# A guess dealt out in single operations over ScalarE, in the second step of a sparse-attention graph layer

## The chip, the core and the metric

One core of a Trainium2 chip runs the kernel. The metric is device time in microseconds (us). Engines are named as in the profile: PE (TensorE, matrix products and transposes), DVE (VectorE), ACT (ScalarE), POOL (GpSimd), SP (SyncE, which issues DMAs).

## What is computed

The input is x (3327 nodes, 256 features) and a sparse matrix adj. After a layer norm and a ReLU, two steps run; each has an attention over all nodes that keeps, for every row, the largest probabilities until their sum passes 0.9:

```
q = X @ W1.T @ W2.T ;  k = X @ W3.T
probs = softmax(q @ k.T)                 # one row per node
keep the largest probs of a row while the sum of those before is < 0.9
A = kept probs / their sum
for n in range(2):
    A  = top_p_attention(Xa)
    Xf = R @ Xf          # R: adj + identity, rows scaled to sum 1
    Xa = A @ Xa
    Z  = Z + Xf @ U1[n].T + Xa @ U2[n].T
out = x + layernorm(X + Z) * g + b
```

## The kernel before

The 3327 nodes are padded to 26 tiles of 128 rows; "a row" below is one such tile, and e is its 128 x 3328 array of exponentials. Every row goes through the same stages, which are Python generators, and the stages of neighbouring rows are interleaved.

`weights` makes e: PE multiplies query and keys (L591), and ACT takes the Exp of four quarters (L601 for three, L609 and L611 for the fourth with its last column apart); the sums go to the columns of `za`.

`measured_twice` (second step) finds a first threshold. It begins with `guessed`: on ACT, small operations on 128 x 1 columns of a tile g, each reading the one before it (L621 to L626), and two more, L675 and L676. POOL then forms three columns (L677 to L679). Now come three passes of ACT over the whole e, each line L634 with a sum per row: one Relu and one Sign at the guessed threshold, then, after two small ACT operations (L688, L689) that read DVE's L686 and L687, a second Sign at a better threshold. DVE (L698, L700, and L706 to L717), POOL (L690 to L693) and ACT (L702 to L704) compute from the three sums a last value, and ACT's L719 makes of it the column that the next stage compares with.

`settle` finds the exact threshold on DVE: a pass over e (L734), 20 searches for the eight largest of a piece (L739), rounds of search and replacement (L746, L750), and a last pass over e (L776) that sets to zero what is not kept.

`Sums` transposes e on PE in pieces of four tiles (pt, L822), copies them on ACT (eT, L824) and multiplies with the nodes (pa, L836). `spread` multiplies the gathered neighbours (pr, L942), and `finish` (L991 on) makes the output row. In the opening of the second step the last rows of the first are closed (L959 to L962), and `laws` computes on PE and DVE constants for all rows (L548 to L554).

The order of each engine's queue is the order of the text, and that is written by hand: each row has seven parts, and for each part a string of letters says which generator is advanced by one yield. In the second step w is `weights` two rows ahead, m `measured_twice` of the next row, n what is left of it from the row before, d `settle`, f `finish`, s `spread`, l `laws`, g the fetching of neighbours; `PLAN[1]` holds the strings of the rows that repeat, `OPEN` those of the first rows, `LAST` those of the last.

Of the kernel before, what the change touches and what calls it, by code (L numbers as in the profile page):

```python
# [9 lines left out]
F32 = mybir.dt.float32  # L10
# [3 lines left out]
AF = mybir.ActivationFunctionType  # L14
# [4 lines left out]
P = 128  # L19
# [327 lines left out]
def guess_graph_layer(ctx, tc, x, adj, w1t, w2t, w3t, u1t, u2t, ln_g, ln_b, out, flag):  # L347
# [9 lines left out]
    small = ctx.enter_context(tc.tile_pool(name="small", bufs=4))  # L357
# [5 lines left out]
    V, G, S, PE = nc.vector, nc.gpsimd, nc.scalar, nc.tensor  # L363

    rows_of = lambda t: min(P, N - t * P)
    valid = lambda t: 0 <= t < NT
# [206 lines left out]
    def weights(step, t, live, known=True):  # L573

        r = dict(Z=rec[:, step, 3, t : t + 1])
        qT = asked(t)
        yield
        r["ms"] = law_of(t) if known and step else early.get(t)
        lawful = law_once(step, t) if known and not step else none
        r["e"] = e = es[(2, 3, 0, 1, 4, 5)[t % 6] if step else t % 4]  # L580
        r["za"] = za = small.tile([P, CUT + 1], F32, tag="za", name="za")
        live[step, t] = r
        w = HALF * P
        wd = w // CUT
        pls = {}

        def product(n):
            pls[n] = pl = ps_l.tile([P, 2, 512], F32, tag="pl", name="pl")
            for a in range(2):
                p = slice(a * DA, (a + 1) * DA)  # L590
                PE.matmul(pl[:, a, :wd], qT[p, :],  # L591
                          keys_of(step, a).rearrange("p a b -> p (a b)")[:, n * wd : (n + 1) * wd],
                          start=True, stop=True)

        for n in range(CUT):
            c = n * wd
            if n not in pls:
                product(n)
            pl = pls.pop(n)
            if n < CUT - 1:  # L600
                S.activation(e.rearrange("p (a n) -> p a n", a=2)[:, :, c : c + wd], pl[:, :, :wd],  # L601
                             AF.Exp, accum_out=za[:, n : n + 1])
                if known and not step and n < 2:
                    r["ms"] = returned(lawful) if n else next(lawful)
                if known and step and n == CUT - 2:
                    product(n + 1)
                yield
            else:
                S.activation(e.rearrange("p (a n) -> p a n", a=2)[:, :, c : w - 1], pl[:, :, : wd - 1],  # L609
                             AF.Exp, accum_out=za[:, n : n + 1])  # L610
                S.activation(e[:, w - 1 : w], pl[:, 0, wd - 1 : wd], AF.Exp, accum_out=za[:, n + 1 :])  # L611

    def guessed(r, g, step):

        r["col"] = col = lambda k: g[:, k : k + 1]
        ms = r["ms"]  # L620
        S.activation(r["za"], r["za"], AF.Copy, accum_out=r["Z"])  # L621
        S.activation(col(0), r["Z"], AF.Ln)
        S.activation(col(2), col(0), AF.Relu, scale=-0.25, bias=ms(7))
        S.activation(col(2), col(2), AF.Exp, scale=-1.0, bias=con((6, 9)[step]))
        S.activation(col(3), col(2), AF.Square, bias=con((3, 8)[step]))
        S.activation(col(9), col(3), AF.Exp, scale=ms(3), bias=ms(8))  # L626
        return col

    def con(k):
        return one[:, k : k + 1]  # L630
# [5 lines left out]
    def measured_once(r):  # L636
        e, ms = r["e"], r["ms"]


        col = guessed(r, small.tile([P, 17], F32, tag="g", name="g"), 0)  # L640
        S.activation(col(4), col(2), AF.Square, bias=con(4))
        S.activation(col(11), col(4), AF.Identity, scale=ms(5), bias=ms(6))
        S.activation(col(1), col(0), AF.Exp, scale=-1.0, bias=con(5))
# [25 lines left out]
    def measured_twice(r):  # L669
        e, ms = r["e"], r["ms"]  # L670

        col = guessed(r, small.tile([P, 18], F32, tag="g", name="g"), 1)
        S.activation(col(1), col(0), AF.Exp, scale=-1.0, bias=con(5))  # L675
        S.activation(col(11), col(2), AF.Square, bias=con(4))  # L676
        G.tensor_scalar(col(11), col(11), ms(5), ms(6), ALU.mult, ALU.add)  # L677
        G.tensor_scalar(col(5), col(1), OFFSET[1], None, ALU.mult)  # L678
        G.tensor_scalar(col(7), col(3), ms(3), ms(8), ALU.mult, ALU.add)  # L679
# [6 lines left out]
        V.tensor_scalar(col(3), oa[:, 1:2], float(NP), col(9), ALU.add, ALU.mult)  # L686
        V.tensor_scalar(col(4), col(3), 0.5, oa[:, 0:1], ALU.mult, ALU.subtract)  # L687
        S.activation(col(6), col(4), AF.Ln, scale=col(1), bias=con(2))  # L688
        S.activation(col(13), col(6), AF.Exp, scale=col(11), bias=col(7))  # L689
        G.tensor_scalar(col(14), col(13), col(9), 0.25, ALU.add, ALU.mult)  # L690
        G.tensor_scalar(col(10), col(13), col(5), 1.0, ALU.mult, ALU.add)
# [8 lines left out]
        V.tensor_scalar(d1, col(15), col(4), 0.0, ALU.add, ALU.max)  # L700
        V.tensor_scalar(col(0), oa[:, 2:3], NP - 61.0, BIG, ALU.is_gt, ALU.mult)
        S.activation(col(2), d1, AF.Abs, scale=col(1), bias=con(1))  # L702
        S.activation(col(2), col(2), AF.Ln, scale=0.2, bias=col(10))
        S.activation(col(3), d1, AF.Ln, scale=col(1), bias=con(2))  # L704
        yield
        V.tensor_scalar(col(12), col(4), d1, 1.0e-30, ALU.subtract, ALU.add)  # L706
# [258 lines left out]
    def first_end(t):  # L965
        if t >= NT - ENDS:
            last = t == NT - 1
            aT = adjp.tile([P, AD, P], F32, tag="at", name="aT", bufs=2)[:, :ND, :] if last else None
            aT = transposed(live.pop(("r", t)), xT=aT, copy=V.tensor_copy if last else S.copy)
            ends.append((t, aT))  # L970
            stores()
            yield
            yield from prep(aT, t, V.tensor_copy if last else S.copy)
            return
        aT = transposed(live.pop(("r", t)))
        stores()
        yield
        pz = ps_r.tile([P, 2 * D], F32, tag="pr", name="pz")
        for c in range(ND):
            PE.matmul(pz, aT[:, c, :], u2[:, c].rearrange("p n d -> p (n d)"), start=c == 0, stop=c == ND - 1)  # L980
        S.copy(xw[:, t, :], pz[:, D:])
        sv = row.tile([P, D], F32, tag="sv", name="sv", bufs=2)
        S.copy(sv, pz[:, :D])
        G.tensor_tensor(sv, sv, x0[:, t, :], ALU.add)
        yield
        kept[t] = sv
        yield from prep(aT, t)
# [36 lines left out]
    none = iter(())  # L1024
# [3 lines left out]
    def run(work, n=99):  # L1028
        for _ in range(n):
            next(work, None)  # L1030
# [137 lines left out]
    def refetch(t):  # L1168
# [7 lines left out]


    ROUNDED = "dsdfdfddfd"
    CLOSED = "mdmwdmdmdmdmdmd"
    PLAN = (("gmdsssa", "gmcdsssa", "edawwpg", "gmsdga", "gmspdea", "ohgdawwqg", "gehmgq"),  # L1180
            ("llcmss", "lnms", "lwwnfd", "lcmdsssgggg", "fdmwqd", "llm" + ROUNDED, "l" + CLOSED + "g"))

    LAST = {NT - 1: ("cfss", "cn", "nd", "sss", "f" + "d" * 5 + "sdf" + "d" * 11, "ff", ""),
            NT: ("c", "", "", "ff", "ff", "ffv", "f"),
# [4 lines left out]
             NT + 1: ("", "weweee", "", "", "", "", ""),  # L1189
             2: ("gmdsssa", "gmcdsssga", "gedawwpg", "gmsdga", "gmspdea", "ohgdawwqg", "gehmgq")}  # L1190
    OPEN = {-1: ("mxx", "mxl", "mxlggg", "mgxl", "mwxl", "m" * 7 + "l", "lmlggg"),
            0: ("cmssggg", "lnms", "wwnfd", "cmdsss", "fdmgwqd", "m" + ROUNDED, CLOSED),
            1: ("cmss", "nms", "wwnfd", "cmdsssgggg", "fdmwqd", "mg" + ROUNDED, CLOSED + "g")}
    OPEN[2] = OPEN[3] = OPEN[1]
    spacing = itertools.chain(spaced((0, 1)), *(spaced((t,)) for t in range(2, NT)))
    fetching = itertools.chain(*(refetch(t) for t in range(NT)))
# [22 lines left out]
    for step in range(2):  # L1219
        sums = Sums(step, live, xw if step else x0, AHEAD[step])  # L1220

        for i in range(-1, NT + 2):
# [4 lines left out]
            if step == 1 and i == -1:  # L1227
# [6 lines left out]
                m=measured(step, live[step, i + 1]) if valid(i + 1) else none,  # L1234
                s=spread(step, i - 2 + 2 * step) if valid(i - 2 + 2 * step) and (step or i < NT) else none,
                w=later.pop((step, i + 2), none),
                e=first_end(i - 2) if step == 0 and valid(i - 2) else none,
                a=itertools.islice(lister, 6) if step == 0 else none,
                p=packed(i + 1) if step == 0 and i >= 0 and valid(i + 1) else none,
# [112 lines left out]
```

## Time and profile before

| | |
|---|---|
| median of 3 runs | 1324.24 us (1319.92 to 1325.54) |
| the profiled execution | 1318.72 us, span 1316.6 us |
| second step, rows that repeat | from 795.5 to 1250.2 us of the span |
| busy share of the span | PE 95%, DVE 87%, ACT 81%, POOL 69% |

Times in the profile are us from the span's start. A row of a timeline reads: start, duration, engine, line, operation, what is written <- what is read, shape, count, and in brackets the idle time before it with what ended it. A small operation's duration can reach into the next one's start, so that the distance of two starts says what an operation takes of its engine; the chain of waits shows it cut in this way. A matmul of 32-bit values is counted twice.

### The profile page before, as it was taken

To read this page: it belongs to the slowest core of one execution; us is meant where nothing else is said; L and a number is where in the kernel's file an instruction comes from. 1 tells how busy PE (TensorE), PEld (TensorE's weight loads), DVE (VectorE), ACT (ScalarE), POOL (GpSimd) and SP (SyncE) were. 2 spreads that over 40 slices of the span, in tenths; PEclk is the share of its full clock that TensorE was granted. 3 is DMA by queue.
4 is the path that set the end of the run, shared out by engine and by line. 5 is a ranking of instruction groups with operands and counts; after the bars stand their busy time and mean duration, and the time that the engine had idled before them with its cause. 6 is when DMAs were issued, how large, how long until landed. Compare 5 with 4: busy or idle time off the path is not lost.

```text
span 1316.6 us, 22157 instructions
## 1 busy us (share of the span) xinstructions
PE 1254.5 (95%) x6396; PEld 958.4 (73%) x6396; DVE 1141.8 (87%) x3674; ACT 1070.2 (81%) x2304; POOL 914.7 (69%) x1226
## 2 busy tenths in 40 slices
PE   5989899999999999999999869999999999999995
PEld 4635677777877778777777547877777777777874
DVE  6867799999999999999994499899998999989993
ACT  5375788798888888888873779999999999999951
POOL 6114788888878888888785466776776767677632
PEclk9999999999999999999999969999999999999998
DMA  7734555455555555554533321322313222131200
GB/s 249 264 118 137 156 143 148 139 158 149 145 149 149 145 161 136 144 161 143 151 87 104 94 70 51 105 68 84 96 55 101 62 89 93 59 100 56 91 21 23
DMA packets 100723, 153.13 MB, mean 116 GB/s; under 512 B 16849, under 2 KB 67152, under 8 KB 100592
## 3 DMA queue, kind: packets, MB, share of 16 engines
q1 hardware_dynamic: 83056, 108.72, 26.0%
q0 software_dynamic: 16640, 42.69, 12.9%
q8 instruction: 53, 0.87, 0.3%
q14 instruction: 78, 0.64, 0.2%
q10 hardware_dynamic: 896, 0.21, 0.1%
HBM read 120.88 MB, written 27.28 MB: 113 GB/s over the span
## 4 chain that ended last, share of the span: by engine, by line
PE 54%; ACT 33%; DVE 8%; issue 2%; POOL 1%; DMA 0%; DVEq 0%; ACTq 0%; POOLq 0%; SPq 0%
PE pa L836 23%; ACT ja L634 15%; PE pl L591 8%; PE pt L822 6%; PE pr L942 5%; ACT eT L824 4%; PE pz L980 3%; ACT e L601 3%; PE pz L1053 3%; ACT x L601 1%; DVE cand L739 1%; PE pk L1097 1%; DVE w L734 1%; PE pk L481 1%; ACT e L609 1%
## 5 line engine op out<-in xcount | busy, mean ns | idle before, releaser
L634 ACT ACTIVATE ja<-e,g 128x3328 uint8<-128x3328 f32 x106 | 325.7, 3073 | 0.2
L836 PE MATMUL pa<-xw,eT 128*128 128x256 f32 x1352 | 321.3, 382 | 3.1 <-DVE s L991 3.1
L836 PE MATMUL pa<-x,eT 128*128 128x256 f32 x1352 | 321.7, 379 | 0.1
L836 PEld LDWEIGHTS pa<-xw,eT 128*128 128x128 f32 x1352 | 250.8, 190 | 48.8 <-DVE cand L739 13.2
L836 PEld LDWEIGHTS pa<-x,eT 128*128 128x128 f32 x1352 | 242.8, 190 | 25.9 <-ACT xa L845 0.4
L739 DVE MAX8 cand<-w 128x8 f32<-128x168 f32 (+1 forms) x1040 | 253.3, 317 | 0.0
L824 ACT COPY eT<-pt 128x512 f32<-128x512 f32 (+1 forms) x364 | 198.5, 553 | 44.7 <-PE pt L822 43.0
L913 POOL DMA_INDIRECT ac<-in_adj,index x130 | 187.8, 1444 | 58.1 <-issue 17.6
L934 POOL DMA_INDIRECT xg<-bx,index x130 | 184.1, 1416 | 48.1 <-issue 16.9
L822 PE MATMUL pt<-ident,e 128*128 128x128 f32 x1144 | 176.2, 276 | 6.3 <-DVE e L773 2.9
L822 PEld LDWEIGHTS pt<-ident,e 128*128 128x128 f32 x1144 | 138.5, 143 | 59.9 <-issue 33.1
L734 DVE SCALAR_TENSOR_TENSOR w<-e,g 128x3328 f32<-128x3328 f32 x44 | 162.5, 3692 | 1.0
L934 POOL DMA_INDIRECT xg<-vx,index x130 | 128.8, 991 | 34.3 <-issue 25.1
L942 PE MATMUL pr<-xg,ac 128*128 128x257 f32 (+1 forms) x520 | 141.5, 396 | 11.0 <-DVE s L1161 7.0
L776 DVE SCALAR_TENSOR_TENSOR e<-e,rec 128x3328 f32<-128x3328 f32 x40 | 147.2, 3680 | 0.6
L601 ACT ACTIVATE e<-pl 128x832 f32<-128x832 f32 x132 | 113.9, 865 | 28.2 <-PE pl L591 28.2
L942 PEld LDWEIGHTS pr<-xg,ac 128*128 128x128 f32 x520 | 93.5, 194 | 38.8 <-issue 15.4
L591 PE MATMUL pl<-both,qT 64*128 64x416 f32 x416 | 99.6, 543 | 7.7 <-ACT e L601 4.3
L591 PE MATMUL pl<-after,qT 64*128 64x416 f32 x416 | 89.5, 544 | 0.0
L678 POOL TENSOR_SCALAR g<-g 128x1 f32<-128x1 f32 x26 | 83.5, 3213 | 1.8
L866 DVE TENSOR_REDUCE fm<-at 128x4 f32<-128x512 f32 (+1 forms) x133 | 84.3, 634 | 0.0
L677 POOL TENSOR_SCALAR g<-g,law 128x1 f32<-128x1 f32 x23 | 25.1, 1093 | 81.3 <-ACT g L676 81.3
(273 smaller groups left out, 2052.1 us busy)
## 6 DMA issues: line engine op xcount, KB each, us to landing
at<-in_adj SPq DMA_DIRECT2D x114, 256.0 KB
cx<-ac SPq DMA_DIRECT2D x26, 384.0 KB
ac<-cx SPq DMA_DIRECT2D x26, 384.0 KB
wide<-in_adj SPq DMA_DIRECT2D x8, 832.0 KB
e<-in_adj SPq DMA_DIRECT2D x6, 832.0 KB
own<-bx SPq DMA_DIRECT2D x26, 128.5 KB
x<-in_x SPq DMA_DIRECT2D x13, 256.0 KB
qT<-both SPq DMA_DIRECT2D x104, 32.0 KB
```

The costliest lines, as they stand in the source:

```text
L591: PE.matmul(pl[:, a, :wd], qT[p, :], keys_of(step, a).rearrange("p a b -> p (a b)")[:, n * wd : (n + 1) * wd], start=True, stop=True)
L601: S.activation(e.rearrange("p (a n) -> p a n", a=2)[:, :, c : c + wd], pl[:, :, :wd], AF.Exp, accum_out=za[:, n : n + 1])
L634: S.activation(ja, e, f, bias=guess, scale=sign, accum_out=total)
L734: V.scalar_tensor_tensor(w, e, col(16), e, ALU.is_lt, ALU.mult, accum_out=d2)
L739: V.max(cand[:, 8 * s : 8 * s + 8], w[:, s * SEG : min(NP, (s + 1) * SEG)])
L776: V.scalar_tensor_tensor(e, e, at(1), e, ALU.is_ge, ALU.mult, accum_out=ra)
L822: PE.transpose(pt[:, j, :], e[:, (j0 + j) * P : (j0 + j + 1) * P], ident)
L824: S.copy(eT[:, :w, :], pt[:, :w, :])
L836: PE.matmul(self.pa, eT[:, c - 4 * k, :], self.xa[:, j, :], start=c == 0, stop=c == NT - 1)
L913: G.indirect_dma_start(out=ac[:, k, :], out_offset=None, in_=rows, in_offset=bass.IndirectOffsetOnAxis(ap=index[:, t, k : k + 1], axis=0), ...
L934: G.indirect_dma_start(out=xg[:, k, :w], out_offset=None, in_=rows, in_offset=bass.IndirectOffsetOnAxis(ap=index[:, t, k : k + 1], axis=0))
L942: PE.matmul(pr[:, :w], ac[:, k, :], own if k == KT - 1 else xg[:, k, :w], start=k == 0, stop=k == KT - 1)
```

## The change

Only the second step is touched. What `guessed` did there is now a generator of its own, `guessing`, with one operation per yield; `weights` makes it when the fourth Exp is issued. A new letter z advances it, for the row two ahead. The operations are the same eight, with the one that makes column 1 moved into the middle and the last two swapped; their lines are now L619 to L632. In `measured_twice` there are more yields: the first resumption runs what is left of the first six operations, the second the last two and POOL's three; the Ln and the Exp of the old L688 and L689 (now L716 and L718) stand in two resumptions, as do the old L702, L703 and L704 (now L731, L733, L735). The old L719 is L750. In part 4 the strings now resume w twice, with one m between them, so that the fourth Exp comes there and no longer in part 6. The first step computes what it did before.

```diff
@@ weights: at its end
+                if step:
+                    r["chain"] = guessing(r)
+
+    def guessing(r):
+        r["col"] = col = lambda k, g=small.tile([P, 18], F32, tag="g", name="g"): g[:, k : k + 1]
+        ms = r["ms"]
+        S.activation(r["za"], r["za"], AF.Copy, accum_out=r["Z"])
+        yield
+        S.activation(col(0), r["Z"], AF.Ln)
+        yield
+        S.activation(col(2), col(0), AF.Relu, scale=-0.25, bias=ms(7))
+        yield
+        S.activation(col(1), col(0), AF.Exp, scale=-1.0, bias=con(5))
+        yield
+        S.activation(col(2), col(2), AF.Exp, scale=-1.0, bias=con(9))
+        yield
+        S.activation(col(3), col(2), AF.Square, bias=con(8))
+        yield
+        S.activation(col(11), col(2), AF.Square, bias=con(4))
+        S.activation(col(9), col(3), AF.Exp, scale=ms(3), bias=ms(8))
+
+    def guess_of(t):
+        for _ in live[1, t]["chain"]:
+            yield
@@ measured_twice
-        col = guessed(r, small.tile([P, 18], F32, tag="g", name="g"), 1)
-        S.activation(col(1), col(0), AF.Exp, scale=-1.0, bias=con(5))
-        S.activation(col(11), col(2), AF.Square, bias=con(4))
+        chain = r.pop("chain")
+        if "col" not in r:
+            run(chain, 5)
+        next(chain)
+        col = r["col"]
+        yield
+        run(chain)
...
         S.activation(col(6), col(4), AF.Ln, scale=col(1), bias=con(2))
+        yield
         S.activation(col(13), col(6), AF.Exp, scale=col(11), bias=col(7))
...
         S.activation(col(2), d1, AF.Abs, scale=col(1), bias=con(1))
+        yield
         S.activation(col(2), col(2), AF.Ln, scale=0.2, bias=col(10))
+        yield
         S.activation(col(3), d1, AF.Ln, scale=col(1), bias=con(2))
@@ the strings
-    CLOSED = "mdmwdmdmdmdmdmd"
+    CLOSED = "zmdmzmzdmmdmdmdmdmd"
-            ("llcmss", "lnms", "lwwnfd", "lcmdsssgggg", "fdmwqd", "llm" + ROUNDED, "l" + CLOSED + "g"))
+            ("llcmnmss", "lms", "lwwnfd", "lcmdsssgggg", "fdwmwmqd", "llzmz" + ROUNDED, "l" + CLOSED + "g"))
-            0: ("cmssggg", "lnms", "wwnfd", "cmdsss", "fdmgwqd", "m" + ROUNDED, CLOSED),
-            1: ("cmss", "nms", "wwnfd", "cmdsssgggg", "fdmwqd", "mg" + ROUNDED, CLOSED + "g")}
+            0: ("cmmssggg", "lnms", "wwnfd", "cmdsss", "fdwmgwmqd", "zmz" + ROUNDED, CLOSED),
+            1: ("cmnmss", "ms", "wwnfd", "cmdsssgggg", "fdwmwmqd", "zmzg" + ROUNDED, CLOSED + "g")}
@@ where the generators are set
+                z=guess_of(i + 2) if step and i > 0 and valid(i + 2) else none,
```

ACT in a row that repeats, from its second pass to its third; before, the two small operations come first and one Exp (the third) after them:

```order
L634 ACTIVATE ja,oa<-e_100,g 128x3328
L824 COPY eT<-pt 128x512
L688 ACTIVATE g<-g,one 128x1
L689 ACTIVATE g<-g 128x1
L601 ACTIVATE x_95,za<-pl 128x2x416
L824 COPY eT<-pt 128x512
L634 ACTIVATE ja,oa<-e_100,g 128x3328
```

and now:

```order
L658 ACTIVATE ja,oa<-e_100,g 128x3328
L855 COPY eT<-pt 128x512
L601 ACTIVATE x_95,za<-pl 128x2x416
L716 ACTIVATE g<-g,one 128x1
L609 ACTIVATE x_95,za<-pl 128x2x415
L611 ACTIVATE x_95,za<-pl 128x1
L718 ACTIVATE g<-g 128x1
L855 COPY eT<-pt 128x512
L619 ACTIVATE za,rec<-za 128x5
L658 ACTIVATE ja,oa<-e_100,g 128x3328
```

Third and fourth Exp and the sum over `za` of the row two ahead now stand between the two passes.

ACT behind the third pass, before:

```order
L824 COPY eT<-pt 128x512
L702 ACTIVATE g<-g,one 128x1
L703 ACTIVATE g<-g 128x1
L704 ACTIVATE g<-g,one 128x1
L609 ACTIVATE x_95,za<-pl 128x2x415
L611 ACTIVATE x_95,za<-pl 128x1
L824 COPY eT<-pt 128x512
L621 ACTIVATE za,rec<-za 128x5
L622 ACTIVATE g<-rec 128x1
L623 ACTIVATE g<-g,law 128x1
L624 ACTIVATE g<-g,one 128x1
L625 ACTIVATE g<-g,one 128x1
```

and now:

```order
L621 ACTIVATE g<-rec 128x1
L855 COPY eT<-pt 128x512
L623 ACTIVATE g<-g,law 128x1
L731 ACTIVATE g<-g,one 128x1
L625 ACTIVATE g<-g,one 128x1
L733 ACTIVATE g<-g 128x1
L627 ACTIVATE g<-g,one 128x1
L735 ACTIVATE g<-g,one 128x1
L855 COPY eT<-pt 128x512
L629 ACTIVATE g<-g,one 128x1
L750 ACTIVATE g<-g 128x1
L631 ACTIVATE g<-g,one 128x1
```

The operations of the guess (L621 to L632) alternate with those of the row one ahead and with copies.

DVE in the opening of the second step, where the law pieces run; before, behind the third pass of row 0:

```order
L698 TENSOR_SCALAR g<-oa,g 128x1
L700 TENSOR_SCALAR g<-g 128x1
L701 TENSOR_SCALAR g<-oa 128x1
L706 TENSOR_SCALAR g<-g 128x1
L707 TENSOR_SCALAR g<-rec,g 128x1
L709 RECIPROCAL g<-g 128x1
L711 TENSOR_SCALAR g<-g 128x1
```

and now:

```order
L727 TENSOR_SCALAR g<-oa,g 128x1
L729 TENSOR_SCALAR g<-g 128x1
L730 TENSOR_SCALAR g<-oa 128x1
L737 TENSOR_SCALAR g<-g 128x1
L738 TENSOR_SCALAR g<-rec,g 128x1
L551 COPY wide<-pq 128x3x65
L552 COPY law<-pq 128x3
L554 SCALAR_TENSOR_TENSOR wide,law<-pq,wide 128x65 x3
L551 COPY wide<-pq 128x3x65
L552 COPY law<-pq 128x3
L554 SCALAR_TENSOR_TENSOR wide,law<-pq,wide 128x65 x3
L740 RECIPROCAL g<-g 128x1
```

Two groups of law pieces now come before the reciprocal of row 0. PE's queue and SP's are unchanged; POOL's is unchanged but for two places of the opening.

More of the change, by code (lines that the diff above doesn't have):

```diff
@@ L611, in weights, with guessed @@
                 S.activation(e[:, w - 1 : w], pl[:, 0, wd - 1 : wd], AF.Exp, accum_out=za[:, n + 1 :])
-    def guessed(r, g, step):
+                if step:
[20 more added lines that the diff above has]
+            yield
+    def guessed(r, g):
         r["col"] = col = lambda k: g[:, k : k + 1]
@@ L623, in guessed @@
         S.activation(col(2), col(0), AF.Relu, scale=-0.25, bias=ms(7))
-        S.activation(col(2), col(2), AF.Exp, scale=-1.0, bias=con((6, 9)[step]))
-        S.activation(col(3), col(2), AF.Square, bias=con((3, 8)[step]))
+        S.activation(col(2), col(2), AF.Exp, scale=-1.0, bias=con(6))
+        S.activation(col(3), col(2), AF.Square, bias=con(3))
         S.activation(col(9), col(3), AF.Exp, scale=ms(3), bias=ms(8))
@@ L637, in measured_once @@
         e, ms = r["e"], r["ms"]
-        col = guessed(r, small.tile([P, 17], F32, tag="g", name="g"), 0)
+        col = guessed(r, small.tile([P, 17], F32, tag="g", name="g"))
         S.activation(col(4), col(2), AF.Square, bias=con(4))
```

## The prediction, made before the changed kernel ran

> **What bounds the kernel now.** The change touches only the second step (rows from 760 us on), so I read in this order: the page's chain of waits, the busy time of the stretch in which the second step repeats, then one row of it engine by engine. The chain's shares by engine, and the stretch (its columns: PE, PEld, DVE, ACT, POOL busy us, PE clock, DMA share, GB/s):
>
> ```profile
> PE 54%; ACT 33%; DVE 8%; issue 2%; POOL 1%; DMA 0%; DVEq 0%; ACTq 0%; POOLq 0%; SPq 0%
> 795.50:1250.20 454.70, 449.76 (x2334) 353.29 (x2333) 415.80 (x1388) 436.94 (x837) 327.92 (x417) 1.00 0.26 80
> ```
>
> PE is busy 98.9% of the stretch, ACT 96.1%, DVE 91.4%: three engines in step, and the question is how far apart they are. The chain in order of time for one row (start, us, what) runs over ACT alone, but for two short trips to DVE:
>
> ```profile
> 939.25 3.06 ACT ja L634 x2
> 942.30 0.95 ACT eT L824 x2
> 943.25 1.70 ACT x L601 x4
> 944.95 3.06 ACT ja L634 x2
> ...
> 948.60 0.39 ACT g L688
> ...
> 949.08 0.39 ACT g L689
> ...
> 950.31 0.48 ACT eT L824
> 950.79 3.07 ACT ja L634 x2
> ...
> 954.61 0.39 ACT g L702
> ...
> 955.09 0.29 ACT g L703
> ...
> 955.66 0.84 ACT x L609 x2
> 956.50 0.15 ACT x L611 x2
> ...
> 957.12 0.21 ACT za L621 x2
> ...
> 957.59 0.30 ACT g L623
> ...
> 958.57 0.39 ACT g L626
> 958.96 0.18 ACT g L675
> 959.14 0.18 ACT g L676
> 959.33 0.26 ACT eT L824
> 959.58 0.29 ACT g L719
> ```
>
> So ACT sets the row of 20.62 us. PE's own timeline says how much that costs; its eight transposes (pt x8) open a row, its sixteen products (pa x16) close it:
>
> ```profile
> 792.06 3.61 PE L836 MATMUL pa<-xw,eT 128*128 128x256 f32 x16
> 795.51 1.04 PE L822 MATMUL pt<-ident,e 128*128 128x128 f32 x8
> ...
> 939.84 1.06 PE L822 MATMUL pt<-ident,e 128*128 128x128 f32 x8
> 956.67 3.61 PE L836 MATMUL pa<-xw,eT 128*128 128x256 f32 x16
> 960.46 1.06 PE L822 MATMUL pt<-ident,e 128*128 128x128 f32 x8 [0.18 <-DVE e L776]
> ...
> 1250.18 1.06 PE L822 MATMUL pt<-ident,x 128*128 128x128 f32 x8
> ```
>
> At 792.06 the closing products were followed by the next row after 3.45 us, without a wait; at 956.67 after 3.79. So PE lost 0.34 us waiting for DVE's last pass over e, and its own row is 20.62 - 0.34 = 20.28 us. That is the floor of everything that follows: the 22 rows from 795.51 to 1250.18 took 454.67, at 20.28 each they take 446.2. **At most 8.5 us can be won in these rows, however much ACT saves.**
>
> **The change part by part.** (1) ACT's row. What it removes is no instruction: the same 14 small ones stand in other places. Those that follow the one whose result they read cost 0.30 to 0.39 (L623, L626); those whose neighbour is independent cost 0.18 (L675, L676), and 0.29 where the scale is a column too (L719). In the new order hardly one stands behind its own source. New row: three passes 3 x 3.06 = 9.18; six copies of 0.48 and one of 0.26, 3.14; the Exps 1.70, twice 0.84 (L609 and, of its size, the third) and 0.15, 3.53; two instructions of 0.21, six of 0.18, six of 0.29, 3.24. Together **19.09** as the lower end. Upper end: the 14 keep what they cost now, 4.1 (the row less 9.18, four copies and a short one, the Exps, the trips of (2) and 0.3 of gaps), and the gaps: 20.25. I take a value near the lower end, 19.2, since the rows with independent neighbours are the nearest.
>
> (2) The two trips. From the second pass's end (944.95 + 3.06 = 948.01) to L688 are 0.59, of which the copy in between covers 0.48; from the third's (953.86) to L702 0.75. In the new order a copy and the third Exp stand before the Ln (0.48 + 0.84), and L621, a copy and L623 before the Abs (0.18 + 0.48 + 0.18 = 0.84): both trips are covered. If that cover were gone they would cost 0.11 and 0.27 per row again.
>
> (3) What becomes longer. The fourth Exp, its one-column tail and the sum of the Exps now stand between the second pass and the third, so second end to third end is 0.48 + 0.84 + 0.29 + 0.99 + 0.29 + 0.48 + 0.21 + 3.06 = 6.64, where it was 953.86 - 948.01 = 5.85. Queued behind it on DVE is L698, and behind that the ten pieces to the last pass over e, for which PE waits. DVE's waits now:
>
> ```profile
> 948.10 0.21 DVE L686 TENSOR_SCALAR g<-oa,g 128x1 f32<-128x1 f32 x1 [1.30 <-ACT ja L634]
> ...
> 953.95 0.27 DVE L698 TENSOR_SCALAR g<-oa,g 128x1 f32<-128x1 f32 x1 [0.16 <-ACT ja L634]
> ...
> 995.92 0.27 DVE L698 TENSOR_SCALAR g<-oa,g 128x1 f32<-128x1 f32 x1 [0.88 <-POOL g L690]
> ```
>
> So DVE alone needs 20.62 - 1.46 = 19.16 a row, 5.69 of it from L686 to L698. I expect its wait to move from L686 to L698, about 0.9 there. The loop that could hold PE up is then: PE's first four transposes 0.6 with the way to ACT, two copies 0.95, two Exps 1.70, second pass 3.06, then 6.64, then 6.60 (953.86 to 960.46) to PE's next transposes: **19.55**, 0.73 under PE's 20.28. With the small ones at their old prices 19.8; below the floor too. So the stall of 0.34 goes, and ACT and DVE wait for PE. On PE the order is unchanged; of ACT's copies for it only the one at 950.31 comes later, by 0.6, and the wait that PE has in the row names DVE, no copy.
>
> (4) POOL. Its order in the repeating rows is unchanged. L678 shows what it is tied to:
>
> ```profile
> L678 POOL TENSOR_SCALAR g<-g x23: 233/3603/3607, 781.5 to 1229.7; 128x1 f32<-128x1 f32 x23
> ...
> 952.15 0.26 POOL L691 TENSOR_SCALAR g<-g 128x1 f32<-128x1 f32 x1
> ```
>
> It takes 0.23 once and 3.60 otherwise, through DVE's pass L734. So POOL is released by that pass, and L691, done 1.5 before L698 needs it, stays tied to DVE. POOL's L690 reads the Exp that now stands behind the fourth Exp; it starts 0.48 + 0.84 + 0.29 + 0.99 = 2.6 after the second pass and ends at 2.9 (L689 began 1.1 after it), and POOL, busy with the output of a row and with transfers, reaches L690, just ahead of the row shown, 3.9 after. Cost nothing; without that cover each 0.1 later would pass to L698. The SP queue is unchanged.
>
> (5) The opening of the second step pays. There row 0 has two Exps (each 0.84 + 0.15) put ahead of its third pass, and DVE meets its scalars one group of law pieces later, a group that ended at 745.5:
>
> ```profile
> 743.14 0.39 ACT L688 ACTIVATE g<-g,one 128x1 f32<-128x1 f32 x1 [2.68 <-DVE g L687]
> 744.04 3.07 ACT L634 ACTIVATE ja<-e,g 128x3328 uint8<-128x3328 f32 x1
> ...
> 745.43 0.08 DVE L554 DVE_READ_ACCUMULATOR wide<-pq,wide 128x1 f32 x1
> ...
> 749.60 0.27 DVE L698 TENSOR_SCALAR g<-oa,g 128x1 f32<-128x1 f32 x1
> ...
> 752.37 1.63 PE L548 MATMUL pq<-qm,both 64*128 64x130 f32 x6 [1.64 <-DVE wide L554]
> ...
> 758.03 3.69 DVE L734 SCALAR_TENSOR_TENSOR w<-e,g 128x3328 f32<-128x3328 f32 x1
> ...
> 767.90 2.93 PE L942 MATMUL pr<-xg,ac 128*128 128x256 f32 x6 [7.02 <-DVE s L1161]
> 773.72 1.94 PE L822 MATMUL pt<-ident,e 128*128 128x128 f32 x8 [2.89 <-DVE e L773]
> ```
>
> L688 moves from 743.14 to about 746.0, and the two Exps add 2.0: the third pass starts at about 748.7 instead of 744.04 and ends 4.7 later, at 751.8. L698 then starts at 751.9, not 749.60; but the six scalars behind L707 now come after the next groups of laws, which gives back some 0.9 (six of about 0.15, an estimate from the DVE rows here), so PE's L548 starts 1.4 later and L734, last behind the laws, too. Row 1's guess behind it adds about 0.2: **+1.6**, between 0 (if the laws wait for PE anyway) and 4.7 (the whole delay passes on). I take 1.6 because DVE's order is known there.
>
> The Trainium skill, "TensorE: Matmul & The Clock Gate", Part 1, says the array drops to half clock after an idle window of about 3.4 us and regains it after a busy one. This trace agrees: after 7.02 and 2.89 idle, the eight transposes took 1.94 instead of 1.06. By that page one more cold window would cost half of 3.4, an estimate of 1.7, and the sum below would be -5.6.
>
> (6) The end of the second step is a DVE chain; DVE reaches it up to 0.73 ahead of PE. Between 0 and -0.7, I take -0.4.
>
> Sum: -8.5 + 1.6 - 0.4 = **-7.3 us** against the profiled 1318.72, so 1311.4. The median shown is 5.5 above the profiled execution; from it, **1316.9**.
>
> **The rivals.** *ScalarE keeps the row* (chance 0.24): the dependent prices stay (20.25) and the uncovered trips return (0.39), so 20.6; half of that way, 20.5 a row against 20.67 on average now, gives -3.7 + 1.6 = -2.1, about 1322. For it: the copies between the small ones wait for PE themselves. Against: L675, L676.
>
> *The opening costs its upper end* (0.10): 4.7 instead of 1.6, and the first row again pays for a cold clock, 795.51 - 773.72 = 21.79 against 20.28, 1.5 more: -7.3 + 3.1 + 1.5 = -2.7, 1321.5.
>
> *POOL takes the place of the pass* (0.06), the slower side: L690, behind the Exp that is behind the fourth Exp, becomes the last that L698 waits for. At 995.92 that happened once, at 0.88; every row would be longer by 0.88 - 0.16 = 0.72: 22 x 0.72 + 1.6 = +17, 1341. It decides once that Exp ends more than 3.9 after the second pass; I have 2.9.
>
> **How the numbers follow.** The forecast has 0.60. About 0.5% (6.6 us) is what a measurement of this kernel can tell from no change, and the forecast lies just beyond, at 1317.6 the border: of its 0.60 I count 0.44 as faster, the more since late POOL rows like 995.92 have room now; with 0.05 from the first two rivals, 0.49. Slower 0.07: the POOL rival and 0.01 of the first. Within: 0.44. The range runs from 1311 (all 8.9 won, no cost in the opening, and runs like the fastest) to 1324 (the first two rivals inside); POOL's case and a little at each end stay out.
>
> **What would show it.** PE's wait before pt x8 in the repeating rows gone and a row of 20.28; ACT idle before its copies, released by PE; L686 without wait, L698 with up to 0.9; small ACT instructions 0.18 or 0.29 apart; L734 of row 0 later by 1.4. Wrong if the row stays above 20.5, if L698 waits for POOL, or if the first transposes of row 0 come over 3 us later.

## The result

Nine executions each: **1316.7 us** (1312.74 to 1320.31) after the change, 1323.3 us (1318.87 to 1325.96) before it, ratio **0.995** with a 95% interval of 0.9931 to 0.997. The prediction was 1316.9.

The two profiled executions do not show it by their totals: 1320.31 us (span 1318.3) after, 1318.72 (span 1316.6) before. The last output of the first step, whose order the change does not touch, was written at 726.49 before and at 734.22 after, 7.73 us later. So the second step is compared from that instruction on: the second step took 1316.6 - 726.49 = 590.1 before and 1318.3 - 734.22 = 584.1 after, **6.0 us less**.

```profile
726.49 0.47 ACT L845 ACTIVATE xa<-pa,ra 127x256 f32<-127x256 f32 x1 [3.46 <-PE pa L836]
```

```profile
734.22 0.48 ACT L876 ACTIVATE xa<-pa,ra 127x256 f32<-127x256 f32 x1 [3.46 <-PE pa L867]
```

(the first is from the timeline of the kernel before, the second from the kernel after; L845 became L876, L822 L853, L836 L867, L734 L765, L776 L807, L686 L714, L698 L727.)

**The profile after.** The chain of waits by engine, and the stretch of the 22 repeating rows (columns as before: PE, PEld, DVE, ACT, POOL busy us, PE clock, DMA share, GB/s):

```profile
PE 79%; ACT 8%; DVE 6%; POOL 2%; issue 2%; DMA 1%; SPq 0%; POOLq 0%; ACTq 0%; DVEq 0%
805.39:1252.31 446.92, 446.00 (x2332) 354.58 (x2333) 417.82 (x1388) 426.09 (x838) 377.04 (x418) 1.00 0.27 81
```

ACT held 33% of the chain before and 8% now; PE is busy 446.00 of 446.92 us, 99.8%. The change moved 22 rows from 454.67 to 446.92. PE's timeline, with a row that starts without a wait, the one late row (ending at 1009.26), and the first and last of the stretch:

```profile
805.39 1.06 PE L853 MATMUL pt<-ident,e 128*128 128x128 f32 x8 [1.18 <-DVE e L807]
825.96 1.07 PE L853 MATMUL pt<-ident,e 128*128 128x128 f32 x8
...
947.55 1.04 PE L853 MATMUL pt<-ident,e 128*128 128x128 f32 x8
948.52 1.67 PE L591 MATMUL pl<-after,qT 64*128 64x416 f32 x8
...
964.35 3.61 PE L867 MATMUL pa<-xw,eT 128*128 128x256 f32 x16
967.80 1.04 PE L853 MATMUL pt<-ident,e 128*128 128x128 f32 x8
...
1009.26 1.06 PE L853 MATMUL pt<-ident,x 128*128 128x128 f32 x8 [0.78 <-DVE x L807]
...
1252.31 1.04 PE L853 MATMUL pt<-ident,x 128*128 128x128 f32 x8
```

From 947.55 to 967.80 a row takes 20.25, and its first transposes come 3.45 after the sixteen closing products, without a wait: PE's own pace. Now the other two engines wait, ACT first:

```profile
948.19 1.08 ACT L855 COPY eT<-pt 128x512 f32<-128x512 f32 x2 [0.64 <-PE pt L853]
949.56 0.87 ACT L601 ACTIVATE x<-pl 128x832 f32<-128x832 f32 x1 [0.29 <-PE pl L591]
...
951.25 3.07 ACT L658 ACTIVATE ja<-x,g 128x3328 uint8<-128x3328 f32 x1
...
957.83 3.09 ACT L658 ACTIVATE ja<-x,g 128x3328 uint8<-128x3328 f32 x1
...
962.26 0.30 ACT L733 ACTIVATE g<-g 128x1 f32<-128x1 f32 x1
962.46 0.28 ACT L627 ACTIVATE g<-g,one 128x1 f32<-128x1 f32 x1
962.65 0.38 ACT L735 ACTIVATE g<-g,one 128x1 f32<-128x1 f32 x1
```

```profile
954.52 0.21 DVE L714 TENSOR_SCALAR g<-oa,g 128x1 f32<-128x1 f32 x1
...
961.12 0.27 DVE L727 TENSOR_SCALAR g<-oa,g 128x1 f32<-128x1 f32 x1 [0.92 <-ACT g L621]
...
963.47 0.15 DVE L748 TENSOR_TENSOR g<-g 128x1 f32<-128x1 f32 x1
...
963.81 3.69 DVE L807 SCALAR_TENSOR_TENSOR e<-e,rec 128x3328 f32<-128x3328 f32 x1
```

ACT idles 0.64 and 0.29 a row, for PE's transposes and for PE's first product of the next Exps, so its own row is 20.25 - 0.93 = 19.32. On DVE, L714 behind the second pass no longer waits (1.30 before, as L686), and L727 behind the third waits 0.92.

### The profile page after: what moved, and what is told of

It is laid out like the page before. It is cut to its first block, busy times and chain, and to the rows that moved or that the text cites. A ratio compares the mean times of both kernels' runs of the same rounds, so it can differ in the third digit from the quotient of the medians.

```text
span 1318.3 us, 22155 instructions
## 1 busy us (share of the span) xinstructions
PE 1254.9 (95%) x6396; PEld 962.5 (73%) x6396; DVE 1144.6 (87%) x3674; ACT 1059.4 (80%) x2304; POOL 967.6 (73%) x1226
## 4 chain that ended last, share of the span: by engine, by line
PE 79%; ACT 8%; DVE 6%; POOL 2%; issue 2%; DMA 1%; SPq 0%; POOLq 0%; ACTq 0%; DVEq 0%
PE pa L867 37%; PE pl L591 11%; PE pt L853 10%; PE pr L973 9%; ACT ja L658 3%; PE pz L1084 3%; PE pz L1011 3%; DVE cand L770 1%; PE pk L1128 1%; ACT e L601 1%; PE pk L481 1%; ACT eT L855 1%; DVE w L765 1%; DVE x L807 1%; DVE e L807 1%
## 5 line engine op out<-in xcount | busy, mean ns | idle before, releaser
L867 PE MATMUL pa<-xw,eT 128*128 128x256 f32 x1352 | 320.0, 381 | 3.0 <-DVE s L1022 3.0
L867 PE MATMUL pa<-x,eT 128*128 128x256 f32 x1352 | 322.6, 380 | 0.1
L867 PEld LDWEIGHTS pa<-xw,eT 128*128 128x128 f32 x1352 | 250.0, 190 | 48.4 <-DVE cand L770 12.6
L867 PEld LDWEIGHTS pa<-x,eT 128*128 128x128 f32 x1352 | 243.4, 191 | 26.1 <-issue 0.4
L944 POOL DMA_INDIRECT ac<-in_adj,index x130 | 184.9, 1422 | 62.4 <-issue 26.8
L853 PE MATMUL pt<-ident,e 128*128 128x128 f32 x1144 | 176.0, 276 | 7.2 <-DVE e L804 2.9
L853 PEld LDWEIGHTS pt<-ident,e 128*128 128x128 f32 x1144 | 139.3, 143 | 58.7 <-issue 29.6
L765 DVE SCALAR_TENSOR_TENSOR w<-e,g 128x3328 f32<-128x3328 f32 x44 | 162.4, 3691 | 1.0
L807 DVE SCALAR_TENSOR_TENSOR e<-e,rec 128x3328 f32<-128x3328 f32 x40 | 147.2, 3680 | 0.6
L705 POOL TENSOR_SCALAR g<-g,law 128x1 f32<-128x1 f32 x23 | 76.7, 3334 | 23.2 <-ACT g L631 23.1
L706 POOL TENSOR_SCALAR g<-g 128x1 f32<-128x1 f32 x26 | 87.0, 3346 | 1.8
```

The source lines that it names most:

```text
L765: V.scalar_tensor_tensor(w, e, col(16), e, ALU.is_lt, ALU.mult, accum_out=d2)
L807: V.scalar_tensor_tensor(e, e, at(1), e, ALU.is_ge, ALU.mult, accum_out=ra)
L853: PE.transpose(pt[:, j, :], e[:, (j0 + j) * P : (j0 + j + 1) * P], ident)
L867: PE.matmul(self.pa, eT[:, c - 4 * k, :], self.xa[:, j, :], start=c == 0, stop=c == NT - 1)
L944: G.indirect_dma_start(out=ac[:, k, :], out_offset=None, in_=rows, in_offset=bass.IndirectOffsetOnAxis(ap=index[:, t, k : k + 1], axis=0), ...
```

## Experiments

All kernels start from the one before or the one after. A **row** below is the distance of two starts of the eight transposes in PE's timeline; the **opening** is from the first product pz of the opening (L990 after the change, L959 before) to the first transposes of row 0: 34.80 us before, 36.33 after. Totals of single executions vary by some 7 us with the first step, so the rows and the opening are read rather than these totals. The times of the experiments come from three chips, each beside the kernel before, so that only the ratios can be set side by side; runs for which no time is given were executed once.

### 1. Only the fourth Exp moved, or the guess in one go

The change has two parts. Guess in one go, in the kernel after (the steps of the last logarithms stay apart):

```
-                z=guess_of(i + 2) if step and i > 0 and valid(i + 2) else none,
+                z=none,
```

> The changed kernel, but a row's guess is no longer dealt out: its first six operations run in one go where the old kernel had them, the fourth Exp and the small operations behind the second and third pass stay where the change put them. My theory (PE's own work of 20.25 us sets the row, ACT has 1.2 us to spare): the guess in one go costs ACT about 0.6 us a row more, ACT's row is 19.7, the row stays at 20.25 to 20.3, and the time is that of the change, 0.5% under before. Rival (dealing out the guess is what won): ACT sets the row again, 20.6, and the time is that of before.

Measured: 1315.08 us, ratio to the kernel before 0.9948 (0.9929 to 0.9966); rows 20.25; opening 36.31. PE's timeline of this kernel:

```profile
824.15 1.04 PE L853 MATMUL pt<-ident,e 128*128 128x128 f32 x8
844.40 1.04 PE L853 MATMUL pt<-ident,e 128*128 128x128 f32 x8
```

Only the fourth Exp moved, in the kernel before:

```
-    CLOSED = "mdmwdmdmdmdmdmd"
+    CLOSED = "mdmdmdmdmdmdmd"
-    ... "fdmwqd" ...
+    ... "fdwmwqd" ...      (and so in the opening's rows)
```

> The kernel before with one part of the change alone: the fourth Exp follows the third with only the two small operations (Ln, Exp) between them, the guess and everything else as before. My theory: the trip to DVE behind the second pass is covered (0.11 to 0.25 us), the one behind the third is not, the guess costs what it did: ACT's own row is about 20.5, still over PE's 20.25, so the rows win some 0.1 to 0.15 each, 2 to 3 us in all, 0.2%. Rival 1 (the place of the fourth Exp is the gain): the whole 0.5%. Rival 2 (the way from the second to the third pass, longer by 0.75 us, costs): slower than before by up to 0.75 a row, 1.2%.

Measured: 1315.35 us, ratio 0.9966 (0.9945 to 0.9988); opening 34.48; rows 20.39. PE's timeline, then DVE's waits in one row:

```profile
839.41 3.61 PE L836 MATMUL pa<-xw,eT 128*128 128x256 f32 x16
842.98 1.07 PE L822 MATMUL pt<-ident,e 128*128 128x128 f32 x8
...
863.37 1.06 PE L822 MATMUL pt<-ident,x 128*128 128x128 f32 x8
```

```profile
1095.85 0.21 DVE L686 TENSOR_SCALAR g<-oa,g 128x1 f32<-128x1 f32 x1 [0.30 <-ACT ja L634]
1102.45 0.28 DVE L698 TENSOR_SCALAR g<-oa,g 128x1 f32<-128x1 f32 x1 [0.91 <-ACT ja L634]
```

The step from 839.41 to 842.98 is 3.57, so PE still waits 0.12. The Exp alone takes 0.23 of the 0.37 us that a row gained, more than the 0.1 to 0.15 of my theory and less than the whole of rival 1, and it leaves the opening as it was; as a whole kernel it cannot be told from the change (the intervals overlap). Without any dealing-out of the guess, rows are as fast as with it, down to 0.01 us. The remaining 0.14 comes from the other cuts that the guess-in-one-go kernel keeps, between the last logarithms, between L716 and L718 and ahead of the guess's last two operations, or from the changed order inside the guess; these were not separated.

### 2. Which engine set the row: TensorE made lighter

In the second step, five of the six products of a row's neighbours are left out (the sum pr then lacks five neighbours), some 2 us of PE. In the kernel before:

```
             PE.matmul(pr[:, :w], ac[:, k, :], own if k == KT - 1 else xg[:, k, :w],
-                      start=k == 0, stop=k == KT - 1)
+                      start=k == 0 or w == D, stop=k == KT - 1)
     (ahead of it: if w == D and k < KT - 1: yield; continue)
```

> The kernel before without five of the six neighbour products of a row in the second step (10 of 12 counted matmuls, 2.2 us of PE a row are left out, so the neighbours' sums are incomplete). My theory: ACT sets the row of the kernel before, so it stays at 20.62 us although PE has only some 18.1 of work. Rival (PE set it already): 18.5 to 19.5.

Measured: rows 20.62, as with all products, PE waiting 1.29 in each for DVE's last pass over e. So the loop over ACT and DVE, and not PE's own work, set the row before. PE's timeline:

```profile
835.32 1.06 PE L822 MATMUL pt<-ident,e 128*128 128x128 f32 x8 [1.29 <-DVE e L776]
855.94 1.06 PE L822 MATMUL pt<-ident,x 128*128 128x128 f32 x8 [1.29 <-DVE x L776]
```

The same edit in the kernel after:

> The changed kernel with the same products left out (2.2 us of PE a row in the second step). My theory: PE sets the row of the changed kernel at 20.25; without these products the loop over PE's transposes, ACT's two copies, two Exps and passes, and DVE's last pass sets it, which the trace of the change puts at 20.0 (its DVE ends 0.27 ahead of PE) and my prediction put at 19.55; ACT's own 19.1 would be the least. Rival (something other than PE holds the changed kernel): the row stays at 20.25.

Measured: rows of two kinds, 20.09 (PE waiting 1.81; my theory had 20.0) and about 21.1. The mean over the 21 rows from 823.31 to 1253.82 is 20.50: with less to do for PE the step became slower. The stretches of two neighbouring rows say where:

```profile
823.30:843.40 20.10, 18.28 (x96) 14.17 (x97) 18.89 (x65) 19.31 (x40) 17.87 (x21) 1.00 0.31 90
843.40:864.50 21.10, 19.96 (x97) 14.88 (x98) 19.02 (x65) 19.44 (x40) 17.25 (x20) 0.92 0.25 78
```

In the long row the granted clock is 0.92 instead of 1.00 and PE is busy 1.65 longer with the same work (19.96 - 18.28, less 0.03 that belongs to the next row, which starts at 864.47). Its timeline:

```profile
843.40 1.06 PE L853 MATMUL pt<-ident,e 128*128 128x128 f32 x8 [1.81 <-DVE e L807]
844.40 2.82 PE L591 MATMUL pl<-after,qT 64*128 64x416 f32 x8
...
864.47 1.07 PE L853 MATMUL pt<-ident,x 128*128 128x128 f32 x8 [1.13 <-DVE x L807]
```

After the wait of 1.81 the eight products for the next Exps took 2.82 instead of 1.67 (as at 948.52 in the kernel after); ACT's first Exp waits for them, and the row goes with it.

To have that loop without the clock, two instead of five products are left out (the sum pr lacks two neighbours):

> The changed kernel, with two of the six neighbour products of each row left out in the second step (the sum pr then lacks the first two neighbours), so that TensorE's own row falls by some 0.78 us to 19.5. It measures the loop over ScalarE and VectorE without much idle TensorE. Theory: a row is VectorE's own 19.2 us plus its waits for ScalarE (0.9 after the third pass), so 20.09 to 20.1, with TensorE waiting 0.6 for the last pass over e, and the granted clock stays at 1.00, since TensorE waits no longer than in the kernel before with fewer products. Rival one, the prediction's own loop: 19.55. Rival two: the clock falls again, and the rows are 21 although TensorE has less to do.

Measured: clock 1.00; of 21 rows 8 took 20.08 or 20.09 and 12 took 20.23 to 20.28, and PE waits 0.5 to 0.7 in these; the row behind 981.14 is late, as in the other kernels. PE's timeline:

```profile
1143.56 1.06 PE L853 MATMUL pt<-ident,e 128*128 128x128 f32 x8 [0.67 <-DVE e L807]
1163.65 1.06 PE L853 MATMUL pt<-ident,e 128*128 128x128 f32 x8 [0.51 <-DVE e L807]
1183.89 1.06 PE L853 MATMUL pt<-ident,e 128*128 128x128 f32 x8 [0.67 <-DVE e L807]
```

So the loop over ACT and DVE, read with PE lightened, is 20.09 in some rows and 20.24 in more of them: 0.16 or 0.01 under PE's 20.25, and not 19.55, which the prediction had. In the kernel after PE starts its rows without a wait and is busy 99.8% of the time, so that PE sets them; but the loop is all but level with it. Where the 0.15 between the two kinds of rows comes from is open; DVE's wait is the same, and its small operation L791 takes 0.46 in the row that ends at 1183.89 and 0.23 in the one before.

### 3. The wait behind the third pass

Five squarings of one column, that nothing reads, between the second and the third pass (behind L718), in the kernel after:

```
         S.activation(col(13), col(6), AF.Exp, scale=col(11), bias=col(7))
+        for k in range(5):
+            S.activation(spare[:, k : k + 1], con(0), AF.Square, bias=con(4))
```

> The changed kernel with five idle squarings of one column (some 0.19 us each, 0.95 a row) put on ACT between the second and the third pass, that is inside the loop over PE, ACT and DVE that the run with fewer products showed at 20.09 us. My theory: the loop becomes 21.05 and sets the row, 0.8 over PE's 20.25, some 17 us in the whole. Rival (ACT has room anywhere, only its sum counts): ACT's sum of 19.3 becomes 20.3, the row stays at 20.25 to 20.35.

Measured: rows 21.01 (823.60 to 844.62 and so on), PE waiting 0.56, DVE behind the third pass 1.83 (L730 is L727 here; the other lines are three higher):

```profile
859.12 0.27 DVE L730 TENSOR_SCALAR g<-oa,g 128x1 f32<-128x1 f32 x1 [1.83 <-ACT g L622]
```

The same five behind the last Exp of the measurement (L750):

> The changed kernel with the same five squarings put behind the last Exp of the row, outside the loop, where ACT waits 0.6 and 0.3 us for PE a moment later. My theory: they fill that wait, the row is 20.25 to 20.35. Rival (every ACT operation costs its time): 21.05 to 21.2, as in the run with the load between the passes.

Measured: rows 20.25 (822.23, 842.48, 862.73). What stands between the second and the third pass passes on beyond the little that PE's row covers; what stands behind the last Exp of the measurement vanishes in ACT's idle time.

### 4. The fourth Exp behind the third pass

The opposite of the change's move: the fourth Exp and the sum behind the third pass, the guess still dealt out.

```
-    ... "fdwmwmqd", "llzmz" + ROUNDED ...
+    ... "fdwmmqd", "llmwzz" + ROUNDED ...     (and so in the opening's rows)
```

> The changed kernel with the fourth Exp (and the sum of the Exps) put behind the third pass instead of before it, so that the two small operations follow the third Exp together, then a copy, then the pass; the guess is still dealt out. My theory: the loop gets about 1.0 shorter (19.1), PE sets the row as before at 20.25, the gain is only where the loop set it: 0.6 in the row behind the opening, and up to 0.8 where one row waits. Time 0.5 to 0.6% under the old kernel, not to be told from the change. Rival (the fourth Exp's place is what gives the gain, as the run with the Exp alone could be read): the gain falls to half.

Measured: 1321.76 us, ratio to the kernel before **1.0019** (1.0007 to 1.0031); rows **20.62**, not 20.25. My theory, by which only the stretch between the passes counts, fell here; and the dealt-out guess with the other cuts wins nothing in the rows while the fourth Exp stands behind the third pass. ACT's and DVE's timelines of one row:

```profile
972.66 3.07 ACT L658 ACTIVATE ja<-x,g 128x3328 uint8<-128x3328 f32 x1
...
975.73 0.85 ACT L609 ACTIVATE e<-pl 128x830 f32<-128x830 f32 x1
...
978.81 0.37 ACT L735 ACTIVATE g<-g,one 128x1 f32<-128x1 f32 x1
```

```profile
975.93 0.27 DVE L727 TENSOR_SCALAR g<-oa,g 128x1 f32<-128x1 f32 x1 [0.53 <-ACT ja L658]
...
979.21 0.16 DVE L748 TENSOR_TENSOR g<-g 128x1 f32<-128x1 f32 x1 [0.88 <-ACT g L735]
```

L735, the last logarithm, starts 978.81 - 972.66 = 6.15 after the start of the third pass instead of 962.65 - 957.83 = 4.82, since the Exp stands ahead of it; and DVE's subtraction L748, the last of the measurement before the pass over e, waits 0.88 for it. In the kernel after it waits for nothing. To ask whether that way or ACT's whole row sets the 20.62, the five squarings behind the last Exp were added to this kernel:

> The changed kernel with the fourth Exp and the sum behind the third pass (rows 20.62), and besides five idle squarings of one column behind the last Exp of the measurement, ahead of the next row's first pass. What sets the 20.62 is open: Theory: the way from the third pass to the last logarithm of the measurement (the fourth Exp now stands in it), for which VectorE waits 0.88 per row before its subtraction; the squarings stand behind that, so rows stay at 20.62 and ScalarE only waits less for TensorE's transposes. Rival: ScalarE's whole row is full, and the wait of VectorE only follows from it; then each row grows by the 0.9 us of the squarings, to 21.5.

Measured: rows 20.62 still. ACT is then busy nearly all the time (432.31 of 440.00 us), yet the row does not move: ACT's whole row is not what sets it. That leaves the way from the third pass to L735 and L748. The stretch of this kernel (columns as before):

```profile
800.00:1240.00 440.00, 434.42 (x2255) 340.62 (x2254) 403.43 (x1327) 432.31 (x917) 338.04 (x399) 1.00 0.26 79
```

One sum serves for the rows that PE does not set: **a row is DVE's own work, 19.2 us, and DVE's waits for ACT; and with all of PE's work in it, it is at least PE's 20.25.** That own work and waits add up to the row is only bookkeeping; what the runs show is that the own part stays the same. With the waits as the rows above and the prediction's show them: before 20.62 - 1.30 - 0.16 = 19.16; Exp alone 20.39 - 0.30 - 0.91 = 19.18; squarings between 21.01 - 1.83 = 19.18; Exp last 20.62 - 0.53 - 0.88 = 19.21; two products fewer 20.09 - 0.91 = 19.18. It does not hold for the longer rows with two products fewer, 20.24 - 0.91 = 19.33, where the open 0.15 comes in.

### 5. The opening in the old steps

Row 0 of the second step alone issued without the new cuts (its guess and its first measurement have no other row to share ScalarE with); here on the kernel with the Exp behind the third pass:

```
-        yield
+        if r["t"]:
+            yield          (at four places of the measurement)
```

> As the run with the fourth Exp behind the third pass, and row 0 is made in the old steps (no added pauses), so that in the opening DVE and ACT keep the old order. My theory: the 1.5 us that the opening of the second step lost come back (36.3 us from the first closing product of the opening to row 0's transposes become 34.8), rows at 20.25: about 0.65% under the old kernel. Rival (the opening waits for PE's laws anyway): nothing comes back.

Measured: 1318.58 us, ratio 1.0002 (0.9989 to 1.0015); opening 34.81 instead of 36.31; rows 20.62. The opening came as my theory had it, the rows and the time did not, for the reason that section 4 gives. So the 1.5 us come from the cut steps of row 0. What they do there is twofold: they put row 0's scalars on DVE behind law pieces, and two Exps ahead of its third pass. The strings of this kernel do not undo that; with row 0 uncut, both Exps follow its third pass again, as before the change. How much each of the two costs was not separated, and the place of these Exps is not ruled out as a cause.

The same on the kernel after:

> The changed kernel, with row 0 of the second step alone issued in the old steps (its guess and its first measurement are not cut up, since no other work stands between them in the opening). Theory: the 1.5 us that the opening lost come back (from the first product pz of the opening to the first x8 product of row 0 34.8 instead of 36.3 us), and the rows stay at 20.25; total 1.5 us under the changed kernel, 0.6% under the kernel before (ratio 0.9935 to 0.994). Rival: the opening's loss comes from the place of the fourth Exp in it, which this kernel keeps; then the opening stays at 36.3 and the ratio at 0.995.

Measured: 1312.93 us, ratio **0.9932** (0.9907 to 0.9956); rows 20.25; opening 35.67, so in this execution 0.66 of the 1.5 came back. The rival of this run was not tested: with row 0 uncut, the two Exps of the opening stand behind the third pass here too.

And with the guess in one go besides:

> As the kernel with row 0 in the old steps, and besides the guess of every row computed in one go at the head of its first section, as before the change. Theory: since the guess in one go cost the rows nothing (20.25) and the old steps of row 0 give back 1.5 us, both together keep both: rows 20.25, opening 34.8, ratio 0.9935 to 0.994, the same as the kernel with row 0 in the old steps alone. Rival: without the dealt-out guess the rows that start the steady state are slower, and the total is 0.5 to 1.5 us more than with it.

Measured: 1312.79 us, ratio **0.9935** (0.9912 to 0.9958); rows 20.25; opening 34.80. PE's timeline of the opening's law products and of the first transposes of row 0 and of row 1, of the kernel with row 0 in the old steps and then of the one with the guess in one go besides (L857 is L853 here, four lines on):

```profile
755.02 1.38 PE L548 MATMUL pq<-qm,both 64*128 64x130 f32 x6 [2.77 <-DVE wide L554]
...
776.12 1.94 PE L857 MATMUL pt<-ident,e 128*128 128x128 f32 x8 [2.89 <-DVE e L808]
...
798.47 1.06 PE L857 MATMUL pt<-ident,e 128*128 128x128 f32 x8 [1.32 <-DVE e L811]
```

```profile
753.36 1.63 PE L548 MATMUL pq<-qm,both 64*128 64x130 f32 x6 [1.64 <-PE pq L548]
...
774.71 1.94 PE L857 MATMUL pt<-ident,e 128*128 128x128 f32 x8 [2.89 <-DVE e L808]
...
796.88 1.06 PE L857 MATMUL pt<-ident,e 128*128 128x128 f32 x8
```

The two openings do not tell the guess in one go from the dealt-out one. Up to row 0's transposes both kernels issue the same instructions in the same order, since no guess is dealt out that early, and they keep time to 0.01 us until this group of law products. It starts 755.02 - 740.45 = 14.57 after the first pz in the one and 753.36 - 739.91 = 13.45 in the other, and row 0's transposes come 0.87 later for it. What delayed it is open. So an opening can differ by 0.9 at one and the same order: with row 0 in the old steps it took 34.80, 34.81 and 35.67, and 0.7 to 1.5 us came back.

From pz to the end of the span the profiled executions took 571.64 (after), 570.61 (guess in one go), 570.95 (row 0 in the old steps) and 569.39 (both); 577.68 before. By these the dealt-out guess costs 1.0 in the first pair and, without the 0.87 of the opening, 0.7 in the second. The times do not tell these kernels apart: their ratios, 0.995, 0.9948, 0.9932 and 0.9935, have intervals that overlap. So dealing out the guess is not shown to win anything, and that it costs a little rests on single executions.

## Why the prediction was right, point by point

**The floor.** Predicted as PE's own row, 20.28: measured 20.25. The 22 rows were to win 8.5 and won 454.67 - 446.92 = 7.75. What is missing stands in the rows that start with a wait: the row that ends at 1009.26 lost 0.78 again, as single rows did before, and the row from 805.39 to 825.96 took 20.57. That ACT set the row before, as the prediction read from the chain, is not the whole of it: ACT was busy 436.94 and DVE 415.80 of the 454.70 us, and each waited for the other.

**(1) ACT's row.** Predicted 19.2, measured 19.32. The small instructions with an independent neighbour do start 0.19 to 0.20 apart (962.26, 962.46, 962.65). The prediction took the dealing-out for a part of the gain; the kernel with the guess in one go shows that the rows are as short without it, as the 0.93 that ACT now idles would suggest. What shortened them is the moved Exp (0.23 a row) and what else the change moved with it (0.14).

**(2) The trips** are covered, as predicted: L716 and L731 wait for nothing in the row shown. Their cover was not taken away by itself; but with the guess in one go L731 waits 0.3 for DVE's L729, and the row stays at 20.25.

**(3) Second pass to third, the loop.** From the second pass's start to the third's it now takes 957.83 - 951.25 = 6.58 (predicted 6.64 between their ends), the wait of DVE moved from L686 to L727 with 0.92 (predicted 0.9). **The loop, 19.55 in the prediction, is 20.09 to 20.24: this term was mis-sized.** Its pieces, by the rows of the kernel after and those of the kernel with five products fewer: PE's first transposes to ACT's copy 0.64 (0.6 predicted); to the start of the second pass 951.25 - 948.19 = 3.06, where the prediction had two copies and two Exps, 0.95 + 1.70 = 2.65; from there to the third pass 6.58; 961.12 - 957.83 = 3.29 to L727, and, in the kernel with five products fewer, 843.40 - 836.90 = 6.50 from L727 to PE's next transposes. Together 20.07. The step that failed is the one that let the first Exp follow the copies directly: it reads PE's first product, which PE makes only behind its eight transposes, and waits 0.29 for it; the starts of the copies and Exps also lie some 0.1 further apart than the sum had. So PE has not 0.73 of room but 0.16 in some rows and 0.01 in others. The forecast held all the same, since a floor hides the size of what is under it; with so little room that was luck, for a loop 0.2 longer would have set the row.

```profile
836.90 0.27 DVE L727 TENSOR_SCALAR g<-oa,g 128x1 f32<-128x1 f32 x1 [0.91 <-ACT g L621]
```

(this row is from the timeline of DVE in the kernel after with five products fewer.)

**(4) POOL** cost nothing: L727 was released by POOL only twice in these rows, 0.9 each, no later than when ACT released it. From the list of waits of the 22 rows (us in total, times, longest):

```profile
DVE g L727 <- ACT g L621: 16.6, 18, 0.9
...
DVE g L727 <- POOL rstd L461: 1.8, 2, 0.9
```

**(5) The opening** was to cost 1.6; from the last output of step one to the first transposes it went from 773.72 - 726.49 = 47.23 to 782.99 - 734.22 = 48.77, **+1.54**. L765 of row 0 came 767.13 - 734.22 = 32.91 after that output, where it was 758.03 - 726.49 = 31.54: 1.37 later, predicted 1.4. The way there was as predicted too: DVE's L727 waits 2.19 there for the third pass, which the two Exps now precede. From the timeline after:

```profile
759.61 0.27 DVE L727 TENSOR_SCALAR g<-oa,g 128x1 f32<-128x1 f32 x1 [2.19 <-ACT ja L658]
...
767.13 3.69 DVE L765 SCALAR_TENSOR_TENSOR w<-e,g 128x3328 f32<-128x3328 f32 x1
...
782.99 1.55 PE L853 MATMUL pt<-ident,e 128*128 128x128 f32 x8 [2.90 <-DVE e L804]
```

Not foreseen: the first row, 805.39 - 782.99 = 22.40 instead of 795.51 - 773.72 = 21.79, 0.6 more. PE waits 1.18 there for row 1's pass over e. The dealt-out guess has a part in it: with the guess in one go the first two rows took 22.17 and 20.28 instead of 22.40 and 20.57. But it is not the whole: with the Exp alone moved, and the guess as before, the first row took 22.50, with a wait of 1.39. The rest was not separated.

One more cold window of PE, which by the prediction's estimate from the Trainium skill ("TensorE: Matmul & The Clock Gate", Part 1) would have made the sum -5.6, was not seen: from the last output of step one to row 0's transposes the granted clock was 0.83, against 0.76 before, and PE's idle time ahead of these transposes is 2.90, against 2.89.

**(6) The end**: predicted -0.4; 1318.3 - 1252.31 = 65.99 against 1316.6 - 1250.18 = 66.42, **-0.43**. The agreement proves little, since the 0.73 from which the 0.4 was taken does not exist; what shortened the end was not looked for.

**Sum**: -7.75 + 1.54 + 0.6 - 0.43 = -6.0, predicted -7.3: 0.75 less was won in the rows, and 0.6 was lost in the first row. The median fell by 6.6. That 1316.9 was met to 0.2 us is luck, since medians of the kernel before alone were 1324.24 and 1323.3.

**The rivals.** ScalarE does not keep the row: PE starts it without a wait, and ACT idles 0.93 a row. The opening stayed near the value taken. POOL did not take the pass's place.

## To carry to other kernels

When three engines run in step, leave out work of one at a time and read the row, together with the granted clock: that shows which engine sets it and how little lies under it. Moving an instruction out of one gap of a measurement puts it into another, so look for the engine that waits for both (here VectorE) and count a row as its own work and its waits. Dealing out a chain of small operations on an engine that idles anyway earned nothing here, and the cuts in the measurement delayed the opening, where no other row covers them. Before a difference of 1 us in one execution is put down to an edit, look whether the two kernels issue the same instructions up to there.

## What the hardware showed that was not expected

**TensorE got slower by having more time.** In the kernel after with five products fewer, PE waited 1.81 a row. After waits of 1.80 us and more the granted clock of the row fell to 0.92 in 7 of 16 rows, and never after waits of up to 1.64; in the kernel after with two products fewer, after one wait of 1.77, and in the kernel before with five fewer, with waits of 1.29, the clock stayed at 1.00. A slow stretch cost 1.65 us of PE. The Trainium skill, "TensorE: Matmul & The Clock Gate", Part 1, has the clock halve after an idle window of about 3.4 us, the window free-running, and rise again after a busy one. By that one window at half clock costs half of 3.4, an estimate of 1.7, with which the 1.65 agrees. The idle time does not agree: here waits of 1.81 to 2.10, little over half of that window, were enough in 7 rows, and waits of 1.80 to 2.13 were not in the other 9.

**The first step varies by 7 us between executions.** The first product of the opening came at 738.92 in the profile before and at 746.66 in that after, with the same order ahead of it; in the other kernels between 739.16 and 745.39. What makes it vary was not looked for. A change of 6 us is seen in the medians and in the parts of one execution, not in the totals of two.
